# The channel stage of a four-layer convolution kernel: spectra as pairs of 64-row products, two-bank PSUM tiles, 120 stationary columns

## The chip, the cores and the metric

The kernel is written in Bass with Tile and runs as one program on one core of a Trainium2 chip. The metric is the device time of one execution in microseconds (us), taken as the median of several runs; less is better. Beside it there is one execution under the hardware profiler, whose page and trace are what the text reads from. In it PE is the matrix engine (matmuls), PEld its weight loads, DVE the vector engine, ACT the scalar engine, POOL and SP the two others; L1546 is a line of the kernel.

## What is computed

The input x has 32 images of 192 channels of 56 x 56 pixels, float32. Four layers follow each other, each x = x + layer(groupnorm(x)), with 32 groups of 6 channels. Layers 0 (attention with agent tokens) and 1 (a recurrence in two directions) mix the channels, and the change does not touch them. Layers 2 and 3 work on each channel by itself:

```python
# layer 2: shift by whole pixels, then a 3 x 3 kernel that is the same for 4 channels
x = x + _L2_conv_ref(_gn(x), L2_conv_offset)
# layer 3: a long convolution (55 x 55, kernel from a small network), through a Fourier transform
y = irfft2(rfft2(x, s) * rfft2(k, s), s)[..., 27:27 + 56, 27:27 + 56]
x = x + (y + bias * x)          # with x normalized on the right-hand side
```

## The kernel before the change

The program runs its stages after each other: the long filter and attention (to some 4.7 ms), the recurrence (to 8.24 ms), and then `channel_blocks`, the stage of the change, which does layers 2 and 3 for all 192 channels in the last 2.13 ms. A channel's 32 images lie in an SBUF tile `x` of 128 partitions: image parity and row (two halves of 64 partitions, 56 of each used) by 16 pairs of images by 56 columns.

The stage makes five products on PE for each channel. The text calls them by letters:

- **R**, `move_rows`: the rows of the normalized tile `xn` are moved and weighted (layer 2, vertical part). 8 matmuls with 112 stationary columns, 112 moving ones. ACT copies the result from PSUM to `across`.
- **C**, `move_columns`: the same for columns, from `across` with 128 stationary columns. DVE adds the result from PSUM into `x` (the step "x") and sums it for the mean.
- **F**, `analyse`: the centred tile `padded` times a matrix of cosines and sines along one image axis. 8 matmuls of 128 rows, 128 stationary and 168 moving columns; the matrix `f1` is block diagonal, its two blocks of 64 rows by 84 columns belonging to the two image parities. ACT copies the result into `y` in 12 pieces.
- **T**, `convolve`: for each of 42 frequencies a Toeplitz product along the other axis, with the tile `toep` that is loaded for the channel (2352 KB). Each product has 32 stationary columns; four run side by side in the four column strips of PE (a quartet). 42 is not a multiple of 4, so the last quartet repeats frequency 41 twice as padding. ACT scales the result by `rs` into `turned`.
- **Z**, `synthesise`: after DVE has transposed `turned` in 32 x 32 blocks into `z` (the step "transpose"), two pairs of matmuls of 64 stationary and 448 moving columns go back to pixels. DVE adds `padded` and writes `done` (the step "done"), which SP sends to the output.

Every float32 matmul appears in the trace as two records. All results pass through PSUM, which has 8 banks of 512 float32 a partition. Before the change a pool hands out eight one-bank tiles, and a channel takes twelve of them: 2 for R, 3 for F, 2 for C, 2 for Z, 3 for T, and a few small ones once in six channels for the mean and the spread. Which bank a tile gets is settled when the program is built.

The products of one iteration of the loop belong to different channels, so that each has time to be ready: in iteration c the loop makes R of channel c + 1, F of channel c - 11, C of channel c, Z of channel c - 13 and T of channel c - 12, in this order on PE. DVE goes in the order: transpose, (mean and fill, once in six), centre (the step "centre", which writes `padded`), x, sum, done, sum of squares. Centre, x and done are `tensor_tensor`. ACT goes: across, y, square, turned, and then issues the load of the next `toep`. POOL normalizes `xn` and builds the small matrices, SP issues the loads of x and the stores. The class `_InOrder` keeps each engine in the order written, so that all instructions of the stage carry its line, L1546; they are told apart by their tiles (`ps<-z` is Z, `ps<-toep` T, `ps<-fixed,padded` F).

Of the kernel before, what the change touches and what calls it, by code (L numbers as in the profile page):

```python
# [30 lines left out]
S = 56  # L31
# [1518 lines left out]
def channel_blocks(ctx: ExitStack, tc: tile.TileContext, taps, k, x2, rs2, spans, out):  # L1550
# [8 lines left out]
    nc = tc.nc  # L1559
    NB = out.shape[0]  # L1560
    NI, NG = NB // 2, NB // 4
    PX = 8 * S
    cp = ctx.enter_context(tc.tile_pool(name="d_c", bufs=1))
    wp = ctx.enter_context(tc.tile_pool(name="d_w", bufs=2))
    sp = ctx.enter_context(tc.tile_pool(name="d_s", bufs=2))
    pp = ctx.enter_context(tc.tile_pool(name="d_p", bufs=8, space=PSUM))
    pe, vector, scalar, pool, sync = (_InOrder(tc, e) for e in (nc.tensor, nc.vector, nc.scalar, nc.gpsimd, nc.sync))
    mm = pe.matmul

# [13 lines left out]
    def kept(name, shape, n):  # L1583
        return [cp.tile(shape, F32, name=f"{name}{i}", tag=f"{name}{i}") for i in range(n)]

    xs, padded = kept("x", [128, NI, S], 10), kept("padded", [128, NI, HALF], 8)
# [7 lines left out]
        nc.vector.memset(t[:, :, S:HALF], 0.0)  # L1594
    for t in turned:
        nc.vector.memset(t[:, :, SLOTS:32], 0.0)

    def psum():
        return pp.tile([128, BANK], F32, name="ps", tag="ps")

    def matrix(n, diff, at, name):

# [62 lines left out]
    def move_rows(c):  # L1665

        xn, rows = normed.pop(c).rearrange("p g w -> p (g w)"), made[c // 4][0]
        moved = across[c % len(across)]
        for i in range(0, NG, 4):
            ps = psum()  # L1670
            for g in range(4):
                mm(
                    ps[: 2 * S, g * 2 * S : (g + 1) * 2 * S], xn[:, (i + g) * 2 * S : (i + g + 1) * 2 * S], rows,
                    start=True, stop=True,
                )
            scalar.copy(
                moved[:, i : i + 4, :, 0:S].rearrange("p g s h -> p (g s) h"),
                ps[: 2 * S, :PX].rearrange("p (n h) -> p n h", h=S),
            )
        return moved  # L1680

    def move_columns(c, moved):

        n, j = divmod(c, GROUP)
        cols, x = made[c // 4][1], xs[c % len(xs)]
        flat = x.rearrange("p g w -> p (g w)")
        for i in range(2):
            ps = psum()
            for g in range(4):
                mm(ps[:, g * 2 * S : (g + 1) * 2 * S], moved[:, 4 * i + g].rearrange("p s h -> p (s h)"), cols[: 2 * S], start=True, stop=True)  # L1690
            px = slice(i * PX, (i + 1) * PX)
            vector.tensor_tensor(flat[:, px], flat[:, px], ps[:, :PX], ALU.add)
        if j == 0:
            groups[n] = Group()
        vector.tensor_reduce(groups[n].sums[:, 0, j], x, AX.X, ALU.add)
# [16 lines left out]

    def find_mean(q):

        ps = psum()
        mm(ps[:, :NI], ones, q.total, start=True, stop=True)
        mm(ps[0:32, NI : NI + 1], q.apart, weight, start=True, stop=True)
        q.mean, q.fill = sp.tile([128, NI], F32, name="mean", tag="mean"), sp.tile([32, 1], F32, name="fill", tag="fill")
        return ps
# [4 lines left out]

    def find_spread(q):
        q.rs = sp.tile([128, 1], F32, name="rs", tag="rs")
        ps = psum()
# [16 lines left out]
        vector.tensor_reduce(groups[n].sums[:, 1, j], sq, AX.X, ALU.add)  # L1744

    def analyse(c):
        y = wp.tile([128, NI, 2, NF], F32, name="y", tag="y")
        _rows_to_spectra(pe, scalar, psum, padded[c % len(padded)], f1, y, NG)
        return y.rearrange("p g s u -> p (g s) u")

    def convolve(c, y):

        q, o, t = groups[c // GROUP], turned[c % len(turned)], toep[c % len(toep)]
        if c % GROUP < len(turned):
            vector.tensor_copy(o[0:32, :, SLOTS], q.fill.to_broadcast([32, S]))
        for a0 in range(0, QUAD, 4):
            n = min(4, QUAD - a0)
            ps = psum()
            for a in range(n):
                for i in range(4):  # L1760
                    u = min(4 * (a0 + a) + i, NF - 1)
                    mm(
                        ps[32 * i : 32 * i + 32, a * 2 * S : (a + 1) * 2 * S], y[:, :, u], t[:, :, 2 * u : 2 * u + 2],
                        start=True, stop=True,
                    )
            scalar.activation(
                o[:, :, 2 * a0 : 2 * (a0 + n)].rearrange("p j (a m) -> p a j m", m=2),
                ps[:, : n * 2 * S].rearrange("p (a j m) -> p a j m", a=n, m=2),
                AF.Copy, scale=q.rs,
            )  # L1770

    def turn(c):
        z = wp.tile([128, 32, S], F32, name="z", tag="z", bufs=1)
# [3 lines left out]
    def synthesise(c, z):  # L1777

        by = z.rearrange("p (g s) j -> p s g j", s=2)
        got = []  # L1780
        for i in range(2):
            ps = psum()
            for s in range(2):
                mm(
                    ps[HALF * s : HALF * s + HALF, :PX].rearrange("p (g w) -> p g w", w=S), back,
                    by[:, s, 8 * i : 8 * i + 8], start=True, stop=True,
                )
            got.append(ps[:, :PX].rearrange("p (g w) -> p g w", w=S))
        return got
# [215 lines left out]
```

## Time and profile before

| | |
|---|---|
| median of 3 runs | 10363.48 us (10363.17 to 10363.57) |
| the profiled execution | 10372.07 us, of which its span 10370.2 us |
| PE busy | 9436.8 us (91% of the span) |
| DVE busy | 9099.9 us (88%) |
| ACT busy | 6324.4 us (61%) |
| POOL busy | 2223.2 us (21%) |
| channel stage | the last fifth: 8242 us to the end (2128 us) |

How to read the views that follow. A line of busy windows has the stretch, its length, then for each of PE, PEld, DVE, ACT and POOL the busy us and (x the number of instructions), then the granted PE clock (1.00 is full speed), the busy share of the 16 DMA engines and GB/s. A line of waits says who waited for whom: us in total, number of times, longest. A group line has the operation, out<-in with its shape and count, then busy us and the mean ns of one, then the engine's idle time just before them and what ended it. A timeline line has start, duration, engine, operation and count, and in brackets the idle time before it and what ended that. Matmul ends are modelled, so PE's busy time can overlap; the spacing of matmul starts is the better measure.

### The profile page before, as it was taken

The page shows a single profiled execution, that of the slowest core. Times are in us where ns is not written, and L with a number is a line of the kernel's source. Part 1 is how long each engine was busy: PE and PEld are TensorE (multiplying, and loading weights), DVE is VectorE, ACT ScalarE, POOL GpSimd, SP SyncE. Part 2 cuts the span into 40 slices and gives each one's busy share as a digit, 9 for nine tenths or more (in the row PEclk, how much of TensorE's full clock was granted, in tenths as well). Part 3 has the DMA queues.
Part 4 walks back from the last instruction along what each step waited for, and adds up shares of the span by engine and source line. Part 5 has one row for each costly group of instructions (what it writes and reads, how often), then busy time and mean ns, then how long its engine had stood idle before and what let it go on. Part 6 is the DMA issues. An engine that isn't in the chain of part 4 may idle for free. (4 is left out here: it accounts for less than half of the span.)

```text
span 10370.2 us, 162899 instructions
## 1 busy us (share of the span) xinstructions
PE 9436.8 (91%) x63814; PEld 5816.8 (56%) x63814; DVE 9099.9 (88%) x11284; ACT 6324.4 (61%) x11964; POOL 2223.2 (21%) x1751
## 2 busy tenths in 40 slices
PE   5999999999999999998888888888888799999998
PEld 3555555655565555555333343333334488888886
DVE  5888888888888888887999999999999788888887
ACT  3555555555555555554566666666666567777777
POOL 0000000000000000000333333333333354554442
PEclk9999999999999999998899999999999899999999
DMA  4212221122112211111244444344444489999999
GB/s 129 68 37 66 68 68 44 58 68 68 47 55 68 68 46 29 49 49 43 69 107 101 103 103 105 104 104 101 101 101 101 129 247 303 307 306 304 304 304 278
DMA packets 1111096, 1247.61 MB, mean 120 GB/s; under 512 B 773091, under 2 KB 813440, under 8 KB 1098232
## 3 DMA queue, kind: packets, MB, share of 16 engines
q1 hardware_dynamic: 914284, 746.65, 28.1%
q10 hardware_dynamic: 196036, 490.46, 13.9%
q8 instruction: 506, 8.29, 0.3%
q14 instruction: 270, 2.21, 0.1%
HBM read 916.15 MB, written 306.43 MB: 118 GB/s over the span
## 5 line engine op out<-in xcount | busy, mean ns | idle before, releaser
L649 DVE SCALAR_TENSOR_TENSOR o<-v_a,att_w,o 128x896 f32<-128x896 f32 (+1 forms) x1024 | 1056.8, 1032 | 422.2 <-ACT v_a L623 301.9
L1167 POOL MEMSET f<- 128x2 f32 x48 | 4.5, 99 | 4751.2 <-DMA st_c<-st 4748.8
L1546 DVE STREAM_TRANSPOSE z<-turned 128x1792 f32<-128x1792 f32 x192 | 680.3, 3543 | 211.2 <-ACT turned L1546 211.2
L1546 ACT COPY y<-ps 64x252 f32<-64x252 f32 (+1 forms) x2304 | 784.6, 341 | 89.6 <-PE ps L1546 59.8
L1161 ACT ACTIVATE pq<-pq 128x784 f32<-128x784 f32 x384 | 329.4, 858 | 676.6 <-DVE pq L1157 676.4
L1153 DVE TENSOR_TENSOR_SCAN pq<-decay,f,both 128x784 f32<-128x784 f32 x384 | 695.7, 1841 | 9.1 <-ACT both L1183 9.1
L1157 DVE SCALAR_TENSOR_TENSOR pq<-both,eu,pq 128x1568 f32<-128x1568 f32 x384 | 701.3, 1840 | 2.0 <-POOL f L1156 0.4
L666 ACT ACTIVATE pr<-ps,low 98x896 f32<-98x896 f32 (+1 forms) x384 | 352.3, 918 | 572.7 <-DVE low L664 572.7
L1153 DVE TENSOR_TENSOR_SCAN pq<-decay,b,both 128x784 f32<-128x784 f32 x384 | 694.1, 1839 | 0.0
L921 PE MATMUL ps<-x,weights 128*128 128x392 f32 x1536 | 584.6, 519 | 83.4 <-ACT x L1141 54.2
L649 DVE SCALAR_TENSOR_TENSOR o<-v_c,att_w,o 128x448 f32<-128x448 f32 (+1 forms) x1024 | 638.6, 624 | 4.9
L662 PE MATMUL ps<-xs_a,gk_a 128*98 128x448 f32 (+1 forms) x1536 | 636.8, 495 | 0.0
L776 ACT ACTIVATE pq<-pq 128x1176 f32<-128x1176 f32 (+2 forms) x224 | 241.9, 1080 | 642.5 <-DVE pq L768 620.5
L663 PE MATMUL ps<-xs_c,gk_c 125*98 125x448 f32 (+1 forms) x1536 | 631.3, 492 | 0.0
L1141 ACT ACTIVATE x<-x,nb,rs 128x784 f32<-128x784 f32 x384 | 386.5, 1030 | 337.3 <-DMA x<-x 183.2
L1546 PEld LDWEIGHTS ps<-toep,y 128*32 128x32 f32 x16896 | 500.4, 151 | 160.9 <-issue 76.0
L763 PE MATMUL ps<-gq_a,xs_a 128*128 128x294 f32 (+1 forms) x1600 | 547.0, 425 | 37.7 <-DVE pq L768 33.1
L1546 PE MATMUL ps<-toep,y 128*32 128x112 f32 x16896 | 560.5, 286 | 12.6 <-DVE done L1546 11.1
L1156 POOL COPY b<-pq 128x2 f32<-128x2 f32 x192 | 394.7, 2056 | 660.9 <-DVE pq L1153 567.3
L1546 POOL TENSOR_TENSOR xn<-x,scale 128x896 f32<-128x896 f32 x192 | 329.7, 1717 | 937.4 <-DMA x<-x 670.5
L764 PE MATMUL ps<-gq_c,xs_c 125*128 125x294 f32 (+1 forms) x1600 | 519.9, 413 | 0.0
L1546 ACT ACTIVATE turned<-ps,rs 128x448 f32<-128x448 f32 (+1 forms) x576 | 377.3, 663 | 223.3 <-PE ps L1546 216.0
(360 smaller groups left out, 23488.2 us busy)
## 6 DMA issues: line engine op xcount, KB each, us to landing
toep<-spans ACTq DMA_DIRECT2D x192, 2352.0 KB
x<-x SPq DMA_DIRECT2D x576, 392.0 KB
x<-x SPq DMA_DIRECT2D x896, 196.0 KB
out_x<-done SPq DMA_DIRECT2D x384, 196.0 KB
spans<-lags SPq DMA_DIRECT2D x24, 2352.0 KB
x<-in_x SPq DMA_DIRECT2D x32, 1568.0 KB
x<-x SPq DMA_DIRECT2D x32, 1568.0 KB
gq_c<-once SPq DMA_DIRECT2D x32, 821.1 KB
```

The costliest lines, as they stand in the source:

```text
L649: nc.vector.scalar_tensor_tensor(dst, tap(i), dww[:, t, i : i + 1], dst, ALU.mult, ALU.add)
L662: mm(ps[P2, h, :n], g[:, cols], xs_a[j][:, px], start=True, stop=False)
L663: mm(ps[P2, h, :n], gk_c[0:KC, 2 * j + h, cols], xs_c[j][0:KC, px], start=False, stop=True)
L666: nc.scalar.activation(pr[:, :, :n], ps[P2, :, :n], AF.Exp, bias=low[:, j, p : p + 1], accum_out=sums[:, j, p : p + 1])
L763: mm(ps[:m, k - q, :HA], xs_a[j][:, px], g, start=True, stop=False)
L764: mm(ps[:m, k - q, :HA], xs_c[j][0:KC, px], gq_c[0:KC, which[k]], start=False, stop=True)
L921: mm(out, aa, srcs[t][h], start=True, stop=False)
L1141: nc.scalar.activation(xs[t], xs[t], AF.Identity, bias=nb1[:, t, s.p : s.p + 1], scale=rs1[:, t, s.p : s.p + 1])
L1153: nc.vector.tensor_tensor_scan(to, decay[:, of(t)].to_broadcast([128, MC]), data, at[:, i : i + 1], ALU.mult, ALU.add)
L1156: nc.gpsimd.tensor_copy(at, z[:, :, last])
L1157: nc.vector.scalar_tensor_tensor(before, both, eu[:, of(t)], before, ALU.mult, ALU.add)
L1546: return lambda *args, **kw: self.tc.keep_in_program_order(do(*args, **kw))
```

## The change

- F becomes 16 products of 64 rows, one for each image parity, 120 stationary and 84 moving columns; the two of a pair lie in the upper and the lower 64 rows of PE and write to different banks. The stationary columns 120 to 127 hold nothing that is used, so only 56 of 64 rows are copied out, and `y` becomes two kept tiles that are set to zero once. ACT's copies go from 12 to 8.
- All PSUM tiles have two banks, and the pool has four of them. R, C and Z take one tile each, F and T two; a channel takes seven. ACT's copy into `across`, DVE's additions into `x` and `done` become one instruction each. T's results come out as 8 quartets in one instruction, then 2 quartets, then half a quartet.
- C uses 120 stationary columns in place of 128, and its addition 120 partitions.
- T leaves out the two padding products; their place in `turned` is set to zero once.

The diff, cut to what is computed:

```diff
-    pp = ctx.enter_context(tc.tile_pool(name="d_p", bufs=8, space=PSUM))
+    pp = ctx.enter_context(tc.tile_pool(name="d_p", bufs=4, space=PSUM))
...
     def psum():
-        return pp.tile([128, BANK], F32, name="ps", tag="ps")
+        return pp.tile([128, 2, BANK], F32, name="ps", tag="ps")
...  move_rows
-        for i in range(0, NG, 4):
-            ps = psum()
-            for g in range(4):
-                mm(
-                    ps[: 2 * S, g * 2 * S : (g + 1) * 2 * S], xn[:, (i + g) * 2 * S : (i + g + 1) * 2 * S], rows,
-                    start=True, stop=True,
-                )
-            scalar.copy(
-                moved[:, i : i + 4, :, 0:S].rearrange("p g s h -> p (g s) h"),
-                ps[: 2 * S, :PX].rearrange("p (n h) -> p n h", h=S),
+        ps = psum()
+        for g in range(NG):
+            mm(
+                ps[: 2 * S, g // 4, g % 4 * 2 * S : (g % 4 + 1) * 2 * S], xn[:, g * 2 * S : (g + 1) * 2 * S], rows,
+                start=True, stop=True,
             )
+        scalar.copy(
+            moved[:, :, :, 0:S].rearrange("p (b g) s h -> p b (g s) h", b=2),
+            ps[: 2 * S, :, :PX].rearrange("p b (n h) -> p b n h", h=S),
+        )
...  move_columns
-        for i in range(2):
-            ps = psum()
-            for g in range(4):
-                mm(ps[:, g * 2 * S : (g + 1) * 2 * S], moved[:, 4 * i + g].rearrange("p s h -> p (s h)"), cols[: 2 * S], start=True, stop=True)
-            px = slice(i * PX, (i + 1) * PX)
-            vector.tensor_tensor(flat[:, px], flat[:, px], ps[:, :PX], ALU.add)
+        ps = psum()
+        for g in range(NG):
+            mm(
+                ps[:ROWS, g // 4, g % 4 * 2 * S : (g % 4 + 1) * 2 * S],
+                moved[:, g].rearrange("p s h -> p (s h)")[:, :ROWS], cols[: 2 * S], start=True, stop=True,
+            )
+        there = x[:ROWS].rearrange("p (b g) w -> p b (g w)", b=2)
+        vector.tensor_tensor(there, there, ps[:ROWS, :, :PX], ALU.add)
...  analyse
-        _rows_to_spectra(pe, scalar, psum, padded[c % len(padded)], f1, y, NG)
+        y, flat = ys[c % len(ys)], padded[c % len(padded)].rearrange("p g w -> p (g w)")
+        for g0, n in ((0, 6), (6, 2)):
+            ps = psum()
+            for g in range(n):
+                at = (g0 + g) * 128
+                for s in range(2):
+                    r = slice(HALF * s, HALF * s + HALF)
+                    mm(
+                        ps[:ROWS, s, g * FREQ : (g + 1) * FREQ], flat[r, at : at + ROWS],
+                        f1[r, s * FREQ : (s + 1) * FREQ], start=True, stop=True,
+                    )
+            got = ps[:, :, : n * FREQ].rearrange("p s (g m u) -> p s g m u", m=2, u=NF)
+            for i in range(2):
+                for m in range(2):
+                    scalar.copy(
+                        y[HALF * m : HALF * m + S, 2 * g0 + i : 2 * (g0 + n) : 2].rearrange("p g s u -> p g s u"),
+                        got[HALF * i : HALF * i + S, :, :, m],
+                    )
...  convolve
-        for a0 in range(0, QUAD, 4):
-            n = min(4, QUAD - a0)
+        for a0, n in ((0, 8), (8, QUAD - 8)):
             ps = psum()
             for a in range(n):
-                for i in range(4):
-                    u = min(4 * (a0 + a) + i, NF - 1)
+                for i in range(min(4, NF - 4 * (a0 + a))):
+                    u = 4 * (a0 + a) + i
...
+            if a0 == 0:
+                scalar.activation(
+                    o[:, :, 0:16].rearrange("p j (b a m) -> p b a j m", b=2, m=2),
+                    ps[:, :, :PX].rearrange("p b (a j m) -> p b a j m", a=4, m=2),
+                    AF.Copy, scale=q.rs,
+                )
+                continue
+            for p, part in ((128, slice(0, n - 1)), (64, slice(n - 1, n))):
+                scalar.activation(
...
...  synthesise and finish
+        ps = psum()
         for i in range(2):
-            ps = psum()
...
-        for i in range(2):
-            g = slice(8 * i, 8 * i + 8)
-            vector.tensor_tensor(y[:, g], t[:, g], got[i], ALU.add)
+        vector.tensor_tensor(
+            y.rearrange("p (b g) w -> p b g w", b=2), t.rearrange("p (b g) w -> p b g w", b=2), got, ALU.add
+        )
```

More of the change, by code (lines that the diff above doesn't have):

```diff
@@ L1562, in channel_blocks @@
     PX = 8 * S
+    ROWS = HALF + S
     cp = ctx.enter_context(tc.tile_pool(name="d_c", bufs=1))
@@ L1596, in channel_blocks @@
         nc.vector.memset(t[:, :, SLOTS:32], 0.0)
+        nc.vector.memset(t[64:128, :, SLOTS - 2 : SLOTS], 0.0)
+    ys = kept("y", [128, NI, 2, NF], 2)
+    for t in ys:
+        nc.vector.memset(t, 0.0)
     def psum():
-        return pp.tile([128, BANK], F32, name="ps", tag="ps")
+        return pp.tile([128, 2, BANK], F32, name="ps", tag="ps")
     def matrix(n, diff, at, name):
@@ L1685, in move_columns @@
         cols, x = made[c // 4][1], xs[c % len(xs)]
-        flat = x.rearrange("p g w -> p (g w)")
-        for i in range(2):
-            ps = psum()
-            for g in range(4):
-                mm(ps[:, g * 2 * S : (g + 1) * 2 * S], moved[:, 4 * i + g].rearrange("p s h -> p (s h)"), cols[: 2 * S], start=True, stop=True)
-            px = slice(i * PX, (i + 1) * PX)
-            vector.tensor_tensor(flat[:, px], flat[:, px], ps[:, :PX], ALU.add)
+        ps = psum()
[6 more added lines that the diff above has]
+        vector.tensor_tensor(there, there, ps[:ROWS, :, :PX], ALU.add)
         if j == 0:
@@ L1713, in find_mean @@
     def find_mean(q):
-        ps = psum()
+        ps = psum()[:, 0]
         mm(ps[:, :NI], ones, q.total, start=True, stop=True)
@@ L1726, in find_spread @@
         q.rs = sp.tile([128, 1], F32, name="rs", tag="rs")
-        ps = psum()
+        ps = psum()[:, 0]
         for i in range(4):
@@ L1746, in analyse @@
     def analyse(c):
-        y = wp.tile([128, NI, 2, NF], F32, name="y", tag="y")
-        _rows_to_spectra(pe, scalar, psum, padded[c % len(padded)], f1, y, NG)
+        y, flat = ys[c % len(ys)], padded[c % len(padded)].rearrange("p g w -> p (g w)")
[13 more added lines that the diff above has]
+                    scalar.copy(
+                        y[HALF * m : HALF * m + S, 2 * g0 + i : 2 * (g0 + n) : 2].rearrange("p g s u -> p s g u"),
+                        got[HALF * i : HALF * i + S, :, :, m],
+                    )
         return y.rearrange("p g s u -> p (g s) u")
@@ L1755, in convolve @@
             vector.tensor_copy(o[0:32, :, SLOTS], q.fill.to_broadcast([32, S]))
-        for a0 in range(0, QUAD, 4):
-            n = min(4, QUAD - a0)
+        for a0, n in ((0, 8), (8, QUAD - 8)):
             ps = psum()
             for a in range(n):
-                for i in range(4):
-                    u = min(4 * (a0 + a) + i, NF - 1)
-                    mm(
-                        ps[32 * i : 32 * i + 32, a * 2 * S : (a + 1) * 2 * S], y[:, :, u], t[:, :, 2 * u : 2 * u + 2],
-                        start=True, stop=True,
-                    )
[L1766 to L1770, printed above, removed]
+                for i in range(min(4, NF - 4 * (a0 + a))):
+                    u = 4 * (a0 + a) + i
+                    mm(
+                        ps[32 * i : 32 * i + 32, a // 4, a % 4 * 2 * S : (a % 4 + 1) * 2 * S], y[:, :, u],
+                        t[:, :, 2 * u : 2 * u + 2], start=True, stop=True,
+                    )
+            if a0 == 0:
[7 more added lines that the diff above has]
+                scalar.activation(
+                    o[:p, :, 16:SLOTS].rearrange("p j (a m) -> p a j m", m=2)[:, part],
+                    ps[:p, 0, : n * 2 * S].rearrange("p (a j m) -> p a j m", a=n, m=2)[:, part],
+                    AF.Copy, scale=q.rs[:p],
+                )
     def turn(c):
@@ L1779, in synthesise @@
         by = z.rearrange("p (g s) j -> p s g j", s=2)
-        got = []
+        ps = psum()
         for i in range(2):
-            ps = psum()
             for s in range(2):
                 mm(
-                    ps[HALF * s : HALF * s + HALF, :PX].rearrange("p (g w) -> p g w", w=S), back,
+                    ps[HALF * s : HALF * s + HALF, i, :PX].rearrange("p (g w) -> p g w", w=S), back,
                     by[:, s, 8 * i : 8 * i + 8], start=True, stop=True,
                 )
-            got.append(ps[:, :PX].rearrange("p (g w) -> p g w", w=S))
-        return got
+        return ps[:, :, :PX].rearrange("p b (g w) -> p b g w", w=S)
     def finish(c, got):
@@ L1793, in finish @@
         t = padded[c % len(padded)][:, :, 0:S][:, :, ::-1]
-        for i in range(2):
-            g = slice(8 * i, 8 * i + 8)
-            vector.tensor_tensor(y[:, g], t[:, g], got[i], ALU.add)
+        vector.tensor_tensor(
+            y.rearrange("p (b g) w -> p b g w", b=2), t.rearrange("p (b g) w -> p b g w", b=2), got, ALU.add
+        )
         for s in range(2):
```

## The prediction

> **What bounds the kernel now.** I read the page's slices first: the channel stage is the last fifth, there the DMA engines and PE are both near full and the PE clock is full. Then three views of a steady stretch of it (8500 to 10200 us): the busy windows, the waits, the groups by form.
>
> ```profile
> 8500.00:10200.00 1700.00, 1671.92 (x23359) 1419.01 (x23358) 1484.58 (x1495) 1293.66 (x2934) 838.31 (x719) 1.00 1.02 305
> ```
> ```profile
> DVE z L1546 <- ACT turned L1546: 164.7, 158, 1.4
> ...
> PEld ps L1546 <- DVE x L1546: 83.0, 137, 1.4
> ...
> PEld ps L1546 <- DVE done L1546: 23.6, 47, 1.0
> ```
> ```profile
> L1546 DVE STREAM_TRANSPOSE z<-turned 128x1792 f32<-128x1792 f32 x160 | 567.4, 3546 | 164.7 <-ACT turned L1546 164.7
> ...
> L1546 ACT ACTIVATE turned<-ps,rs 128x448 f32<-128x448 f32 x320 | 226.7, 715 | 176.8 <-PE ps L1546 172.8
> L1546 DVE TENSOR_TENSOR padded<-x,mean 128x896 f32<-128x896 f32 x160 | 218.0, 1362 | 1.2
> ...
> L1546 DVE TENSOR_TENSOR x<-x,ps 128x448 f32<-128x448 f32 x320 | 191.1, 612 | 18.0 <-PE ps L1546 15.5
> ...
> L1546 DVE TENSOR_TENSOR done<-padded,ps 128x448 f32<-128x448 f32 x320 | 183.1, 613 | 0.0
> L1546 DVE TENSOR_REDUCE sums<-x 128x16 f32<-128x896 f32 x160 | 173.8, 1086 | 5.5
> ...
> L1546 ACT ACTIVATE turned<-ps,rs 128x336 f32<-128x336 f32 x160 | 89.3, 558 | 2.4
> ```
>
> 160 transposes in 1700 us: 10.63 us a channel. PE is busy 98% of it and loses under 1 us a channel to DVE; so PE sets the pace, with DVE (87%) close behind. The waits show where it could tip: PE already waits for DVE to read PSUM tiles empty. The timeline of one channel shows how:
>
> ```profile
> 9013.79 1.12 DVE L1546 TENSOR_TENSOR x<-x,ps 128x448 f32<-128x448 f32 x2
> 9014.43 0.20 PEld L1546 LDWEIGHTS ps<-z,fixed 128*64 128x64 f32 x4 [0.91 <-DVE x L1546]
> ...
> 9015.95 1.14 DVE L1546 TENSOR_TENSOR done<-padded,ps 128x448 f32<-128x448 f32 x2
> 9016.61 1.66 PEld L1546 LDWEIGHTS ps<-toep,y 128*32 128x32 f32 x56 [0.34 <-DVE done L1546]
> ```
>
> The second half of Z waits for DVE's addition into x, the Toeplitz product T for done: their tiles get the banks that were just read. The other half of the same product runs meanwhile, so mostly nothing is lost.
>
> **PE's own work, a channel.** F: 16 matmul records 0.1425 apart (2.30 us) become 16 pairs. The spacing of R is 0.098 (112 stationary columns) and of C 0.112 (128), so 120 columns give 0.105 a pair if the two halves run side by side: 1.68, a gain of 0.62. That they do is shown in the scan stage, where eight loads of 64 rows take what four of 128 rows take:
>
> ```profile
> 5300.51 0.96 PEld L924 LDWEIGHTS ps<-x,weights 64*128 64x128 f32 x8 [0.56 <-issue]
> 5302.03 0.95 PEld L931 LDWEIGHTS ps<-x,weights 128*128 128x128 f32 x4 [0.56 <-issue]
> ```
>
> C: 16 x 0.007 = 0.11 gained. T: 84 records for 88, but the last quartet only becomes two: 0 to 0.1, I take 0.03. Against this F now differs in shape from R before it and C after it; where the shape changes today (T to R, C to Z) the matmul starts lie about 0.2 us further apart than within one shape: two such places, 0.4 lost. Net 0.36 a channel, 65 us over 180 channels. This is not on the path that will set the end, as follows.
>
> **ACT and DVE beside it.** y: 8 copies of 364 ns and 4 of 294 become 4 of about 0.57 (294 plus the slope of 0.83 ns an element) and 4 of 0.29: 0.6 us of ACT gained. across: two of 534 become one of about 0.93. Both are hidden: across, y and the square, 5.4 us by these rows, fit between the end of R and the end of T's first part, some 9 us later in the ring below. SP, POOL and the queues keep their order; DMA gets more time a channel. The new zero fills run once, while DVE waits for the first loads. None of this is on the path.
>
> **The path: waits for PSUM.** Eight tiles of one bank become four of two banks; a channel uses seven where it used twelve. I traced each tile to the last user of its banks in the order of the built program. In 149 of 192 channels Z gets the very pair that C left, and in 117 of those the first part of T gets the pair that Z left. The first matmul there waits for DVE (x, then done), and each of these DVE steps is now one instruction over both banks. So nothing of Z runs beside the addition, nothing of T beside done. Queued behind each wait is all of PE. It closes a ring through turned and the transpose, each leg from the rows above:
>
> - transpose 3.55, then centre (padded) 1.36, in DVE's order;
> - x, 896 elements: between one 896-element reduction (1.09) and two halves (1.22); nearest is the former, 1.09;
> - Z until its reader can start: 1.73 for its 8 matmuls and 0.05, 1.78;
> - done, as x: 1.09;
> - T's first 16 quartets until ACT starts: the first 8 took 1.26 and the next 8 0.93 in the drain (below), 2.19;
> - turned: 896 elements, 0.715 plus 448 x 1.40 ns (the slope between 336 and 448) = 1.34, bounded by two of 558 and two of 715 ns (1.12 and 1.43); then 224 elements 0.40 and 112 elements 0.25, 1.99 together;
> - five handovers, 0.25 together.
>
> Sum 13.3 us. R, F and C take 1.66 + 1.68 + 1.76 + 0.4 = 5.5 after T's 2.85, so C ends 8.4 after T's start; DVE comes to x only 9.2 after it and Z may start at 10.4. PE idles there for 2 us, so its gain disappears. T's second part and the sum of squares lie beside ACT.
>
> Of six channels four go round the whole ring. One, in which T takes another pair, skips done: 3.55 + 1.36 + 1.09 + 1.65 + 2.19 + 1.99 + 0.1 = 11.9. One, in which the mean is found, waits for neither, but the second part of F waits for DVE to copy fill after the transpose: 3.55 + 0.3 + 0.5 + 1.9 + 1.65 + 2.19 + 1.99 = 12.1. Mean (4 x 13.3 + 11.9 + 12.1) / 6 = 12.87, so 2.24 more than 10.63. Times 180 channels 403 us. The drain's ring lengthens too (done before T: about 2 us by some ten channels, 20 us); the fill, which has no T yet, gives a little back. Net 400. The profiled execution took 10372.07 (span 10370.2 and 1.9 around it); that is 8.6 above the median of the runs, which I take off: 10363.5 + 400 = 10765 us.
>
> Bounds: centre was 1.08 when POOL was idle (drain) and 1.6 beside POOL. With 1.08, and turned at its lower bound, the mean ring is 0.4 shorter: 10690. With 1.6: 10800.
>
> **The clock.** PE will idle about 2 us before Z and 1.3 before T. The nearest rows are in the drain and in the scan:
>
> ```profile
> 10263.76 1.73 PE L1546 MATMUL ps<-z,fixed 128*64 128x448 f32 x8 [1.71 <-DVE z L1546]
> ...
> 10265.41 2.85 PE L1546 MATMUL ps<-toep,y 128*32 128x112 f32 x88
> ...
> 10266.67 0.75 ACT L1546 ACTIVATE turned<-ps,rs 128x448 f32<-128x448 f32 x1 [0.80 <-PE ps L1546]
> 10267.60 1.25 ACT L1546 ACTIVATE turned<-ps,rs 128x448 f32<-128x448 f32 x2 [0.19 <-PE ps L1546]
> ```
> ```profile
> 10258.00:10347.00 89.00, 71.39 (x1183) 55.32 (x1174) 59.02 (x46) 67.63 (x161) 0.00 (x0) 1.00 0.96 295
> ```
> ```profile
> 6247.71:6251.12 3.41, 1.05 (x4) 0.30 (x4) 3.41 (x3) 2.95 (x6) 2.89 (x2) 1.00 0.00 0
> 6251.12:6254.53 3.41, 3.41 (x10) 1.52 (x7) 3.41 (x4) 1.07 (x2) 0.45 (x1) 0.50 0.00 0
> ```
>
> Gaps of 1.71 left the clock at 1.00; a stretch with 1.05 of 3.41 us busy was followed by one at 0.50. Ours would hold about 1.4 of 3.41, between the two. If it tips, up to 3.4 us of Z and T run at half speed, 1.7 lost, in perhaps half of the channels: up to 155 us.
>
> The Trainium skill (TensorE: Matmul & The Clock Gate, Why this matters for your kernels) warns only of gaps over about 3 us; by it the sum stays at 10765. The rows speak for an earlier limit, since a gap of 2.36 us was enough at 6248, so I keep both ends.
>
> Against the change stands the Trainium skill (Perfetto Trace Analysis, Optimizing Tensor Performance): matmul groups should rotate through PSUM banks so that one is emptied while the next runs. It has no price; by it alone one expects slower, and nothing above rests on it.
>
> **Rivals.** (1) The ring with clock loss: 10800 to 10930. For it: the 2 us gap. Against: the drain. (2) The halves of F run one after the other: F lasts 1.7 longer (16 x 0.105), C ends 10.1 after T's start where DVE is free at 9.2, and the ring grows by 0.9 in five channels of six, 135 us: 10900. Against: the loads above. (3) Faster: PE keeps setting the pace and its 0.36 shows, at most 65 us: 10300. That needs the ring under 10.3, three us less, so DVE and ACT would have to take their two-bank tiles in a third of the time that their rows say. For it: today's waits cost little, and PE is at 98%. Against: the program's order, and even with centre and transpose off the ring, R, F, C, x, Z, done and T in a row need 5.5 + 1.2 + 1.78 + 1.2 + 2.85 = 12.5. It would also meet DMA, 1.02 busy at 10.63 us. (4) A milder ring: DVE and ACT save more per start-up than the slopes say: 10600 to 10690.
>
> **Numbers.** Ring with clock held 0.55 (10690 to 10800); clock loss 0.28; halves in series 0.05; milder ring 0.06; faster 0.05; no change within 0.2% (about 20 us, what a measurement can tell) 0.01. The range 10660 to 10930 takes in the first three and the top of the fourth.
>
> **What would show it.** Right: in the steady stretch some 12.9 us between transposes; PE near 75% busy; z's matmul idle before it some 2 us by DVE x, T's first 1.3 by DVE done; DVE z waiting for turned; the records of F in pairs about 0.105 apart; DMA share near 0.85; clock 1.00, or below where rival 1 holds. Wrong: PE still over 95% busy, or Z and T starting without a wait for DVE.

## The result and the profile after

The changed kernel takes 10741.44 us (median of 4 runs, 10723.69 to 10754.73) against 10363.33 before (with a fourth run): a ratio of 1.0366, with a 95% interval of 1.0348 to 1.0384. It is slower by 378 us. The profiled execution took 10754.73 us with a span of 10752.9.

The busy windows of the changed kernel over the stretch that was shown of before:

```profile
8500.00:10200.00 1700.00, 1389.02 (x21335) 1135.49 (x21335) 1281.49 (x990) 948.53 (x1803) 716.90 (x611) 0.97 0.83 257
```

PE has gone from 98% busy to 82%, DMA from a share of 1.02 to 0.83, and no other engine has come up: nobody is saturated any more. The engines wait for each other in a circle. The granted clock is 0.97. The waits of the same stretch:

```profile
DVE z L1546 <- ACT turned L1546: 302.7, 133, 4.2
...
PE ps L1546 <- DVE x L1546: 178.9, 113, 2.6
PE ps L1546 <- DVE done L1546: 106.9, 89, 1.6
```

135 channels pass in it. In 113 PE stands before Z for DVE's addition into x (1.58 us each), in 89 before T for done (1.20 each). Before the change these waits were on the weight loads of a product whose other half was running; now PE itself has nothing to do. The groups that answer to those of before:

```profile
L1546 DVE STREAM_TRANSPOSE z<-turned 128x1792 f32<-128x1792 f32 x135 | 475.5, 3523 | 302.8 <-ACT turned L1546 302.7
...
L1546 DVE TENSOR_TENSOR padded<-x,mean 128x896 f32<-128x896 f32 x135 | 206.6, 1530 | 1.0
...
L1546 DVE TENSOR_TENSOR x<-x,ps 120x896 f32<-120x896 f32 x136 | 147.4, 1084 | 25.3 <-PE ps L1546 20.8 <-POOL xn L1546 3.1
L1546 DVE TENSOR_TENSOR done<-padded,ps 128x896 f32<-128x896 f32 x135 | 146.6, 1086 | 82.2 <-PE ps L1546 73.7 <-DMA x<-x 6.4 <-DMA toep<-spans 0.7
...
L1546 ACT ACTIVATE turned<-ps,rs 128x896 f32<-128x896 f32 x135 | 142.0, 1052 | 548.5 <-PE ps L1546 548.5
...
L1546 ACT ACTIVATE turned<-ps,rs 128x224 f32<-128x224 f32 x135 | 60.0, 444 | 0.2
L1546 ACT ACTIVATE turned<-ps,rs 64x112 f32<-64x112 f32 x135 | 45.9, 340 | 0.0
```

The two-bank instructions are cheap. By the busy time of the groups, x takes 1.08 us a channel where its two halves took 1.19, done 1.09 where they took 1.14, the first part of turned 1.05 where two took 1.42. ACT is busy for 7.0 us a channel in place of 8.1; DVE for 9.5 in place of 9.3, since centre takes 1.53 us on average, 1.36 before. That is far from 12.6 us a channel for either. One turn of the ring in the timeline shows what sets the pace:

```profile
9044.37 3.54 DVE L1546 STREAM_TRANSPOSE z<-turned 128x1792 f32<-128x1792 f32 x1 [1.56 <-ACT turned L1546]
...
9047.75 1.08 DVE L1546 TENSOR_TENSOR padded<-x,mean 128x896 f32<-128x896 f32 x1
9048.88 1.09 DVE L1546 TENSOR_TENSOR x<-x,ps 120x896 f32<-120x896 f32 x1
9050.02 1.72 PE L1546 MATMUL ps<-z,fixed 128*64 128x448 f32 x8 [1.23 <-DVE x L1546]
...
9051.80 1.09 DVE L1546 TENSOR_TENSOR done<-padded,ps 128x896 f32<-128x896 f32 x1 [0.71 <-PE ps L1546]
9052.94 2.80 PE L1546 MATMUL ps<-toep,y 128*32 128x112 f32 x84 [1.19 <-DVE done L1546]
9055.19 1.05 ACT L1546 ACTIVATE turned<-ps,rs 128x896 f32<-128x896 f32 x1 [3.94 <-PE ps L1546]
...
9056.84 3.54 DVE L1546 STREAM_TRANSPOSE z<-turned 128x1792 f32<-128x1792 f32 x1 [2.96 <-ACT turned L1546]
```

x, Z, done and T each begin within 0.1 us of the end of the step above. Centre begins 0.16 us before the transpose's end, turned when the first 16 quartets of T are there (0.55 before T's end), and the next transpose after the two small parts of turned that follow the first. So it goes through DVE, PE, DVE, PE, ACT and back: 12.47 us from transpose to transpose. R, F and C, and all that ACT and POOL do besides, lie beside it.

Where the 383 us between the two spans lie, by the starts of R: from the first R to the last 1967 us became 2319 (+351), from the last R to the end (the drain) 140 became 166 (+26), and the first R came 5 us later. The 5 are no mark of the change: over all the profiled executions here the first R came between 8249 and 8276 us. Times of different runs can differ by that much for a reason that lies ahead of the stage.

### The profile page after: what moved, and what is told of

It reads as the page before. It is cut to its first block, busy times and chain, and to the rows that moved or that the text cites. A ratio compares the mean times of both kernels' runs of the same rounds, so it can differ in the third digit from the quotient of the medians.

```text
span 10752.9 us, 166150 instructions
## 1 busy us (share of the span) xinstructions
PE 9415.4 (88%) x66118; PEld 5732.9 (53%) x66118; DVE 9128.1 (85%) x10904; ACT 6116.7 (57%) x11004; POOL 2243.8 (21%) x1751
## 5 line engine op out<-in xcount | busy, mean ns | idle before, releaser
L1546 ACT ACTIVATE turned<-ps,rs 128x896 f32<-128x896 f32 (+2 forms) x576 | 310.5, 612 | 789.5 <-PE ps L1546 789.3
L1546 ACT COPY y<-ps 56x504 f32<-56x504 f32 (+1 forms) x1536 | 668.4, 435 | 129.1 <-PE ps L1546 96.4
L1546 PE MATMUL ps<-z,fixed 128*64 128x448 f32 x1536 | 368.6, 605 | 274.4 <-DVE x L1546 234.7
```

The lines of the kernel that those rows point to most:

```text
L1546: return lambda *args, **kw: self.tc.keep_in_program_order(do(*args, **kw))
```

## The experiments

The theory is the ring: Z and T get pairs of banks that were just written, so they wait until DVE has emptied them. Its rivals: the new products or the two-bank instructions cost the time themselves; the clock does; or something slows a leg of the ring. Ratios are to the kernel before, run on the same chip (where it took 10368 to 10374 us). "A channel" is the mean distance of the starts of R over 160 channels.

### Taking the change apart

**Other banks, the same instructions.** The pool chose the pairs; here they go round:

```diff
...
-        return pp.tile([128, 2, BANK], F32, name="ps", tag="ps")
+        turns.append(None)
+        at = len(turns) % 4
+        return pp.tile([128, 2, BANK], F32, name=f"ps{at}", tag=f"ps{at}")
```

> The changed kernel with the same instructions; only the pair of PSUM banks that a tile gets is changed: the four pairs are handed out in strict rotation, so Z gets the pair that R left, both parts of T get those of F, and nobody gets the pair that was just written. Ring theory: the waits of Z for DVE x and of T for DVE done go, and PE sets the pace again. By the steps of PE in the changed kernel's trace (R 1.76, F 1.84, C 1.75 without its wait, Z 1.65, T 2.71, mean 0.08) that is 9.8 to 10.1 us a channel, 10210 to 10270 us in all, unless DMA (share 1.02 at 10.63 us a channel before) can't follow: then 10300 to 10365. Theory that the two-bank instructions or the paired products themselves cost the time: 10600 or more. Theory that the clock is the main part: the gaps go with the waits, so it can't be told from the ring here.

Measured: 10316.93 us, ratio 0.9945 (0.9928 to 0.9961), 10.21 us a channel. Windows, and the largest of PE's waits for DVE that are left:

```profile
8500.00:10200.00 1700.00, 1660.68 (x26268) 1380.47 (x26266) 1541.52 (x1222) 1169.75 (x2221) 874.47 (x726) 0.99 1.00 317
```
```profile
PE ps L1546 <- DVE fill L1546: 32.3, 28, 1.3
...
PE ps L1546 <- DVE z L1546: 3.9, 2, 2.8
```

The waits for x and done have gone, and with them 425 us: the kernel is now half a per cent faster than before. No instruction of the stage was changed, so neither the products nor the two-bank instructions are to blame; the choice of bank is. The time is above the expectation (10210 to 10270) because of one channel in six, that of the mean: 12.18 us where the others take 9.83. There the rotation gives C the pair that holds the mean, which DVE reads only after the transpose. The expectation had counted that channel like the others; the better version below places that pair elsewhere, and the channel falls to 10.43.

**Only the two-bank tiles.** F, the width of C and the padding as before the change; the tiles, and ACT's and DVE's instructions on them (but for y), as after it, with T's last part in one step:

```diff
-    pp = ctx.enter_context(tc.tile_pool(name="d_p", bufs=8, space=PSUM))
+    pp = ctx.enter_context(tc.tile_pool(name="d_p", bufs=4, space=PSUM))
...
-        return pp.tile([128, BANK], F32, name="ps", tag="ps")
+        return pp.tile([128, 2, BANK], F32, name="ps", tag="ps")
...
```

> The kernel before with only the two-bank tiles: R, C, Z, T and F write pairs of banks (four of them, from the pool as in the change), and across, x, turned and done are one instruction over both; F keeps its 128-row products and its 12 copies, C its 128 columns, T its padding. The bank pattern is the changed kernel's (117 channels with the whole ring). Ring theory: the ring does not contain F or C, so nearly all of the loss is here: 12.4 to 12.7 us a channel, 10690 to 10750 us. If clock loss is a part of the changed kernel's time, this one is a little faster than it, since PE has 0.5 us more work a channel in the shadow of the ring and its gaps are shorter. Theory that the paired products of F are what costs (series, change of shape): near 10363.

Measured: 10737.92 us, ratio 1.0357 (1.034 to 1.0374), 12.57 a channel. Windows and PE's waits for x and done in the same stretch:

```profile
8500.00:10200.00 1700.00, 1424.23 (x19732) 1205.50 (x19731) 1269.01 (x988) 1015.05 (x2209) 721.00 (x611) 1.00 0.83 258
```
```profile
PE ps L1546 <- DVE x L1546: 155.3, 113, 2.1
...
PE ps L1546 <- DVE done L1546: 108.7, 91, 1.6
```

The whole loss is in this half of the change. The granted clock was 1.00 here, so the loss does not need the clock.

**Only the products.** F as pairs, C with 120 columns, T without padding; R, C, Z and T in one-bank tiles:

```diff
-    pp = ctx.enter_context(tc.tile_pool(name="d_p", bufs=8, space=PSUM))
+    pp = ctx.enter_context(tc.tile_pool(name="d_p", bufs=1, space=PSUM))   # ps0 to ps3 in turn, one bank each
+    fp = ctx.enter_context(tc.tile_pool(name="d_f", bufs=2, space=PSUM))   # F's pairs
...
```

> The other half alone: F as pairs of 64-row products into two-bank tiles (two of them, in turn) with 8 copies, C with 120 columns, T without padding products; R, C, Z and T keep one-bank tiles and their instructions in halves, four banks in strict rotation. The last turned copy is split as in the change. Ring theory with PE's own work as measured in the changed kernel's trace (F 0.45 less, C 0.11 less, T 0.05 less): 10.0 to 10.1 us a channel, 10250 to 10275 us; where DMA can't follow, 10300 to 10350. Theory that the paired products cost more than they save: 10363 or more.

Measured: 10285.09 us, ratio 0.9919 (0.9903 to 0.9936), 10.07 a channel. PE is what bounds it, busy for 98.5%, and the halves still help: PE's wait for DVE x is nearly all on its weight loads (114.8 us, against 1.9 on the matmuls). The one-bank tiles go round in four banks here, where the pool chose among eight before. The products make PE's own work 0.43 us a channel shorter (by the starts in the traces of before and of the changed kernel) and the channel is 0.56 shorter, so some of the gain may be the banks'; no run parts the two.

```profile
8500.00:10200.00 1700.00, 1675.15 (x26506) 1381.99 (x26504) 1574.34 (x1562) 1278.36 (x2579) 888.12 (x724) 0.99 1.02 320
```

DMA follows: the share of 1.02 that before showed at 305 GB/s is shown here at 320.

### One wait at a time

With the pairs placed by hand, each wait can be taken away alone. A table gives each tile one of the four pairs p: F0 and F6 are the two parts of F, T0 and T8 those of T; a second table does the channel of the mean, in both runs without its wait for fill. The line taken out below is the pool's own choice in four channels of six, written as such a table. First T's wait:

```diff
-            by = dict(R=p[0], F0=p[1], F6=p[2], C=p[3], Z=p[3], T0=p[3], T8=p[0])
+            by = dict(R=p[0], F0=p[1], F6=p[2], C=p[3], Z=p[3], T0=p[0], T8=p[1])
```

> The changed kernel, pairs placed by hand: Z still gets the pair that C left and waits for DVE x, but the first part of T gets R's pair and no longer waits for DVE done. Ring theory: done (1.09) and its handovers leave the ring, 1.1 to 1.2 us less in the channels that had it; with the mean channel near 10.6 that is 11.3 to 11.6 us a channel, 10510 to 10570 us. Theory that a wait costs what the waits view books on it (done: 127 us of PE idle in 159 channels, 0.8 us each): 10600.

Measured: 10475.58 us, ratio 1.0096 (1.0079 to 1.0113), 11.06 a channel. Then Z's:

```diff
+            by = dict(R=p[0], F0=p[1], F6=p[2], C=p[3], Z=p[0], T0=p[0], T8=p[1])
```

> The converse: Z gets R's pair and no longer waits for DVE x; the first part of T gets the pair that Z left and still waits for DVE done. Ring theory: the ring then runs through DVE alone (transpose, centre, x, the sum of x that until now lay beside Z, done) to T: x plus the sum plus done, 3.27, in place of x, Z and done, 3.95, so only 0.6 to 0.8 less a channel: 11.8 to 12.0, 10600 to 10640 us. Theory that a wait costs what the waits view books on it (x: 207 us of PE idle in 159 channels, 1.3 us each): 10510.

Measured: 10649.66 us, ratio 1.0263 (1.0246 to 1.028), 12.01 a channel. The wait that is left in each:

```profile
PE ps L1546 <- DVE x L1546: 166.3, 129, 2.4
```
```profile
PE ps L1546 <- DVE done L1546: 246.4, 118, 3.5
```

The changed kernel books 178.9 us on x and 106.9 on done, so by the waits taking x away should be worth more. It was the other way round: 266 us came back without done, 92 without x, and some 50 of each belong to the mean's channel (11.95 to 10.2 and 10.35 us, 30 times). Without the wait for x the time moves to done (246.4 us, more than double), since transpose, centre, x, the sum and done follow each other on DVE anyway. The two runs differ in more than the wait: without x, the one channel of six that had skipped done waits for it too (11.13 us became 11.59, 14 us in all), and the half clock costs more there (0.97 against 1.00). The medians of the second and third channel after that of the mean, where most have the full clock and the short centre, are free of that: 12.40 us in the changed kernel, 11.14 without done, 11.60 without x. So done's wait is worth 1.26 us a channel there and x's 0.80, and the order stays. Both results miss their ranges: the first fell 35 us below, since centre also became shorter (1.13 us on average, see the next part) and the mean's channel fell below the 10.6 that was counted; the second lies 10 us above, with the clock at 0.97.

### The legs that were longer than expected

**POOL.** R reads x as loaded; POOL's two steps are left out:

```diff
-        xn = wp.tile([128, NI, S], F32, name="xn", tag="xn")
-        pool.tensor_tensor(xn, x, _bc(scales[n][:, 0], [128, NI, S]), ALU.mult)
-        pool.tensor_tensor(xn, xn, _bc(scales[n][:, 1], [128, NI, S]), ALU.add)
-        normed[c] = xn
+        normed[c] = x
```

> The changed kernel, bank pattern unchanged, without POOL's two steps that scale and shift x (R reads x as it was loaded; this leaves out the normalization). In the changed kernel's trace centre takes 1.55 us on average, 1.08 where POOL is idle and up to 2.45 beside it; in the channels with the whole ring it adds 0.50. If POOL is the cause, centre falls to 1.08 everywhere and the ring channels to 12.4 to 12.7, the mean from 12.60 to 12.15 or so: 10650 to 10680 us. If centre's length comes from something else (DMA, ACT): 10735 to 10745.

Measured: 10633.88 us, ratio 1.0253 (1.0239 to 1.0267), 12.08 a channel; the four kinds of channel with the whole ring take 12.33 to 12.35 each. The group of centre in this run, then centre beside POOL in the timeline of the changed kernel:

```profile
L1546 DVE TENSOR_TENSOR padded<-x,mean 128x896 f32<-128x896 f32 x141 | 154.2, 1093 | 1.0
```
```profile
9011.18 1.69 POOL L1546 TENSOR_TENSOR xn<-x,scale 128x896 f32<-128x896 f32 x1 [3.22 <-DMA x<-x]
9011.37 2.45 DVE L1546 TENSOR_TENSOR padded<-x,mean 128x896 f32<-128x896 f32 x1
9012.95 2.42 POOL L1546 TENSOR_TENSOR xn<-xn,scale 128x896 f32<-128x896 f32 x1
```

Without POOL centre takes 1.09 us, beside it 2.45 at this place. That is worth 108 us here, a little more than expected, because most of the half clock goes with it (0.99): it is the slow centre that makes the wait before Z long enough. The longest such wait is 1.2 us in this run, 2.6 in the changed kernel.

**The clock.** The changed kernel's timeline and window at one such place:

```profile
8863.98 3.07 PE L1546 MATMUL ps<-z,fixed 128*64 128x448 f32 x8 [2.58 <-DVE x L1546]
```
```profile
8863.30:8866.70 3.40, 2.72 (x8) 0.77 (x8) 2.22 (x4) 0.67 (x1) 1.18 (x1) 0.50 0.48 193
```

After a wait of 2.58 us the clock is 0.50, and Z takes 3.07 us in place of 1.72. To price this, idle products fill the waits, in a pair that is free at that time, and the pairs are placed by hand as the pool had placed them; the channel of the mean has none. Nine of them before Z:

```diff
+        if c % GROUP:
+            spare = psum("W")
+            for _ in range(WARM):
+                mm(
+                    spare[:ROWS, 0, :HALF], moved[:, 7].rearrange("p s h -> p (s h)")[:, :ROWS], cols[: 2 * S, :HALF],
+                    start=True, stop=True,
+                )
```

> The changed kernel with the same bank pattern written out by hand, and in five channels of six nine idle products of 120 x 64 (18 records of 0.105 us, 1.9 us) between C and Z, into a free pair that nobody reads: they fill the time in which PE waits for DVE x. The ring is as long as before. Ring theory without clock loss: 10735 to 10750, no change. Clock loss as part of it: the granted clock of the channel stage goes from 0.97 to 1.00 and the time falls by what was lost; some 28 half-clock stretches of 3.4 us in 159 channels lose at most 1.7 us each, 0.3 us a channel, 54 us in all, and half of that if half lies off the ring: 10690 to 10715. If the idle products outlast the wait they cost: over 10750.

Measured: 10771.31 us, ratio 1.0388 (1.037 to 1.0405), clock 0.99. A miss of the design: nine last longer than the wait, from C's start to Z's 3.71 us (median) against 3.17, so the run's time says nothing on the clock. Its legs do: Z and T take 1.77 and 2.26 us in the channels with the whole ring, the full-clock lengths of the table below. With six:

> The run with idle products between C and Z, with six of them in place of nine. Nine (1.9 us) outlasted the wait: from C's start to Z's start 3.71 us in most channels against 3.17 in the changed kernel. Six (1.26 us) end at 3.1, just before. Clock theory: granted clock 0.99 to 1.00, and what the changed kernel lost to half-clock stretches comes back: its channels took 12.62 us on average but 12.40 where the clock was full and centre fast; 0.1 to 0.2 us a channel, 10705 to 10725 us. No clock loss on the ring: 10735 to 10750. If the products themselves disturb the ring: 10750 or more.

Measured: 10745.89 us, ratio 1.0354 (1.0337 to 1.0372), clock 0.98. With six before Z and four between Z and T:

> The run with six idle products between C and Z, and four more (0.84 us) between Z and the first part of T, so that both waits of PE are filled most of the way. In the changed kernel's whole-ring channels Z's leg took 1.95 us and T's 2.33 against 1.77 and 2.25 at full clock. Clock theory: both legs fall to 1.77 and 2.25, 0.26 in four channels of six, 31 us in all: 10700 to 10720 us, granted clock 1.00 in the stage. If half-clock stretches cost the path nothing, 10735 to 10750.

Measured: 10733.79 us, ratio 1.0349 (1.0335 to 1.0363), clock 0.98. Neither reaches the range of the clock theory, but both had the pairs placed by hand. What that costs by itself:

> The changed kernel with its bank pattern written out by hand and nothing else: what the three runs with idle products have to be compared with. Their drain (from the last R to the end) took 180 to 189 us against 166 in the changed kernel, since the hand-written pattern holds there too, where the pool has free pairs; without idle products that should show here as well: 180 us, and 12.55 to 12.65 us a channel before it, 10750 to 10760 us. Then six idle products (10746) gained about 9 us and ten (10734) about 21, and the clock costs the changed kernel some 20 us. If this run is at 10735 to 10745 instead, the idle products gained nothing and the clock costs nothing that can be measured.

Measured: 10760.36 us, ratio 1.0375 (1.0358 to 1.0391), clock 0.97; from the last R to the end 179 us. From the first R to the end it takes 2485 us, as the changed kernel does. Against this control the six gain 14 us and the ten 27, and the intervals of the ratios touch. In the legs of the ring (means of the channels that go all round it) Z and T fall, with the ten, from 2.01 and 2.36 us to 1.88 and 2.26. That is 0.23 in four channels of six, 28 us in 180.

The time does not confirm it. The two profiled executions lie 23 us apart (spans of 10752.2 and 10729.1), and 18 of these lie ahead of the first R, where the programs do the same. From the first R to the end it is 2485 us against 2480: most of what the ring gains is lost again in the channel of the mean, 12.53 us in place of 11.87 (20 us), and in the drain (10 us). Why that channel became longer stays open. So the clock's price is an estimate from the legs, 28 us by this pair of runs, and no run shows it given back in time.

**Both.** POOL's steps left out and the waits filled:

> The two before it together: POOL's two steps left out and both waits filled with idle products. If the ring's sum is complete (transpose 3.52, centre 1.08, x 1.09, Z 1.77, done 1.09, T 2.25, turned 1.05 + 0.56, handovers 0.2), every channel with the whole ring takes 12.40 us and the mean of six is 12.0: 10620 to 10640 us. If clock or POOL cost nothing: as the other run of the two.

Measured: 10662.99 us, ratio 1.0275 (1.0261 to 1.0289), 12.08 a channel, the same as without the idle products. The channels with the whole ring take 12.34 to 12.35 us, against the 12.40 that the sum of legs gave: with POOL gone the clock has nothing more to give. The time misses its range by 23 us and is 29 above the run without POOL's steps. Of these, 18 lie in the drain and 10 ahead of the first R. In the drain the pairs placed by hand alone cost the control 13 us against the changed kernel; the rest there may be the idle products, which no wait covers.

### A better version

The rotation, but in the channel of the mean the pair that holds it goes on to Z, which waits for the transpose in any case:

```diff
+        if c % GROUP == 0:
+            by = dict(R=p[0], M1=p[1], M2=p[2], F0=p[3], F6=p[0], C=p[2], Z=p[1], T0=p[3], T8=p[0])
+            turn_of[:] = p[2], p[1], p[3], p[0]
+        else:
+            by = dict(R=p[0], F0=p[1], F6=p[2], C=p[3], Z=p[0], T0=p[1], T8=p[2])
+            turn_of[:] = p[3], p[0], p[1], p[2]
```

> The run with pairs in strict rotation, with the channel in which the mean is found placed by hand: the mean's pair goes on to Z, which waits for the transposed z anyway, and no longer to C; the other five channels keep the rotation. Ring theory: those five stay at 9.83 us, the sixth falls from 12.18 to 10.4 to 10.8, so the mean falls from 10.21 to about 9.95: 10265 to 10280 us, under the run with the products alone (10285), since the two-bank instructions spare DVE and ACT their second start-up. If DMA or DVE (9.3 us a channel) sets in: 10285 to 10300.

Measured: 10267.21 us, ratio 0.9897 (0.9881 to 0.9914), the fastest of all, though its interval touches that of the products alone. Five channels of six take 9.83 us, the sixth 10.43.

```profile
8500.00:10200.00 1700.00, 1676.07 (x26742) 1390.92 (x26744) 1575.60 (x1237) 1192.88 (x2269) 882.29 (x724) 0.99 1.00 323
```

PE is at 99% and DVE at 93%. From the first R to the end it takes 2006 us, the products alone 2025, the kernel before 2107. So the whole change, with its banks placed, takes some 100 us off the stage.

## Why the prediction was right, step by step

Slower, by the ring, was right, and 10741 is 24 us under the 10765. That it came so close is in part luck: in the ring turned, the transpose and the handovers were 0.69 us too long in the sum, centre, Z and T 0.53 too short, and the two nearly cancel. The ring's legs, as means over the 84 channels of 126 (8500 to 10100 us) that go all round it, from the starts and ends in the trace; in the last column the run without POOL's steps:

| leg | predicted | measured | without POOL's steps |
|---|---|---|---|
| transpose | 3.55 | 3.38 until centre starts | 3.38 |
| centre | 1.36 | 1.58 | 1.08 |
| x | 1.09 | 1.08 | 1.09 |
| Z until its reader | 1.78 | 1.95 | 1.77 |
| done | 1.09 | 1.09 | 1.09 |
| T until ACT | 2.19 | 2.33 | 2.25 |
| turned | 1.99 | 1.62 | 1.61 |
| handovers | 0.25 | 0.10 | 0.11 |
| sum | 13.3 | 13.13 | 12.36 |

- **x, done, the half legs from the drain:** right to 0.06. Taking the lower bound (one reduction) for a two-bank step was right.
- **turned** was over by 0.37. The slope between 336 and 448 elements, stretched to 896, gave 1.34 for a step that takes 1.05, less than the lower bound of 1.12; and the three parts overlap, so that 1.05, 0.44 and 0.34 take 1.62 from first start to last end.
- **centre** was under by 0.22. The sum took the mean of before. There, from 8500 us on, 81 of 171 run beside a POOL step and take 1.65 us on average, the others 1.08; in the changed kernel 92 of 173 do, and take 1.86. The run without POOL's steps shows that POOL is the cause.
- **Z and T** were right at full clock (1.77 and 2.25 in the last column); in the changed kernel they are 0.26 longer together, which is the clock term that the forecast left at zero.
- **The channels outside the ring:** 11.13 for the one that skips done (11.9 predicted) and 11.95 for the mean's (12.1). With them the mean is (4 x 13.13 + 11.13 + 11.95) / 6 = 12.60, against 12.87; over 180 channels 49 us less than predicted. The drain gave some of that back: +26 us, where 20 were predicted.
- **PE's own work** fell by 0.43 a channel, 0.36 predicted: F from 2.30 to 1.84, R from 1.66 to 1.76, C unchanged, T from 2.79 to 2.72. The change of shape costs some 0.1 us at three places (R to F, F to C, and C's first step) and not 0.2 at two. The 0.2 was misread: before the change, the last start of C and the first of Z lie 0.205 us apart and those within C 0.112, so this change of shape adds 0.09; from T to R it is 0.210 against 0.031, 0.18 more. C's gain of 0.11 is gone in it. That this work is off the path was right; the run with the products alone is where it shows.
- **The idle times:** 1.58 us before Z (2 predicted), 1.20 before T (1.3). PE is 82% busy, not 75%: the ring is shorter, and at half clock PE's work takes longer. DMA's share is 0.83 (0.85).
- **Rival 1, the clock,** holds in part: 0.97, not the 1.00 of the forecast, and some 30 us by the legs (0.26 in 120 channels), far from the 155 that were its upper end. It needs a third party, since the waits become long enough where POOL slows centre.
- **The rule on rotating PSUM banks** (the Trainium skill, Perfetto Trace Analysis, Optimizing Tensor Performance), which the prediction held against the change, agrees with the runs: the same instructions take 425 us less with the pairs in rotation.
- **Rival 2** fell: F's pairs run side by side, 1.84 us for 32 records. **Rival 3** (PE keeps the pace) was wrong of the changed kernel and right of the same instructions in other banks. It had asked for DVE and ACT steps in a third of their time; other banks were enough, since they take x and done out of the path rather than shorten them. **Rival 4** (a milder ring) had a point in turned, which saved more than its slope said; what centre and the clock added kept the time above its 10690, and without POOL's steps it is 10634.

## What to carry to other kernels

Merging tiles into larger ones saves start-ups on the readers, but halves the number of tiles: look up which reader frees the buffer that the next writer gets, and follow that chain until it closes, before adding up any savings. If it closes, its sum is the pace, however idle the engines are, and giving the buffers out in another order may give it all back, as it did here without a change to any instruction. A wait's booked time is not its worth; what it is worth shows only when one sums the path that is left without it.

## What the runs showed that was not expected

- DVE's centre (two SBUF tiles in, 896 elements) takes 1.08 us alone and up to 2.56 beside POOL's steps; x, which reads PSUM and came next beside the same POOL step as the centre shown (from 9013.74), took 1.07. The prediction knew of 1.6 beside POOL, but not that the ring would bring more of it. On the ring this was the largest single correction: 108 us came back without POOL, together with the clock.
- The Trainium skill (TensorE: Matmul & The Clock Gate, Why this matters for your kernels) warns of PE gaps over about 3 us. In the changed kernel (8500 to 10100 us) there are 16 half-clock stretches of 3.4 or 6.8 us: 13 came with a wait of 1.9 to 2.6 us, three after one of 1.2. So on this evidence the limit is lower, and not a matter of one gap's length alone: 20 other waits of 1.9 us or more were followed by none, and in the run without POOL's steps two waits of 1.2 us in most channels mostly left the clock at 1.00.
- DMA was not at its limit at a share of 1.02: the same loads and stores ran at 323 GB/s with a share of 1.00 in the better version, where before had 305 at 1.02.
